# Resident tiles last, bank by bank, and the work on single nodes in groups of four tiles

## The chip, the cores and the metric

The kernel runs on one core of a Trainium2 chip. The metric is the device time of one execution in microseconds (us). Every execution leaves records, so each run also gives its span and the clock that TensorE was granted.

## The reference, cut to what matters

Four graph layers over N = 2708 nodes of 128 features share one dense adjacency matrix A (2708 x 2708, float32). 2708 rows are 21 full tiles of 128 and one of 20.

```python
# layer 0: z from A, the 4 nearest neighbours of z, then A plus those neighbours
z  = leaky_relu(lap_mul(A, x) @ W1 + b1, 0.1)
S  = exp(-sqrt(dist2(z, z)) / 2), kept for the 4 nearest of each row, else 0
x  = layernorm(x + lap_mul(S + A, x) @ W2 + b2)
# layer 1: attention; num = A @ exp(leaky_relu(row + col)); H = A @ (att @ XW)
x  = layernorm(x + H)
# layer 2: normalized A times x, a linear layer
x  = layernorm(x + (d * (A @ (d * x))) @ W.T + b)
# layer 3: A times x beside x itself, a linear layer, relu
x  = layernorm(x + relu(concat(x, A @ x) @ W.T + b))
```

So there are five products with A of 128 columns ("passes": two in layer 0, one each in layers 1, 2 and 3), one more for the attention, a search for neighbours with a gather of their rows, and the attention's own stage ("heads").

## The kernel before

Six of the 22 tiles of A stay in SBUF (`res`), sixteen are streamed in each pass through three buffers. A pass sums into six PSUM banks of 512 columns, `accs`; two spare banks (`mis`) serve all small products. Resident and streamed tiles alternate, and all banks end together:

```python
def adj_times(y, extra=None):
    accs = [acc_tile() for _ in range(C)]
    for n, i in enumerate(order):            # two streamed, one resident, ...
        src = res[:, i, :] if i < RES else load_strip(i)
        for c in range(C):
            nc.tensor.matmul(accs[c][:, : cw[c]], lhsT=y[: pw[i], i, :], rhs=src[...],
                             start=(n == 0), stop=(n == T - 1 and extra is None))
    for c in range(C):
        if extra is not None:
            extra(c, accs[c])
        evacuate(c, hT[...], accs[c][...])   # VectorE and ScalarE in turn
```

The work on single nodes follows for all tiles at once; for the end of layer 0 and the gather before it:

```python
for t in range(T):                 # 22 tiles x 4 neighbours = 88 gathers by GpSimd
    for k in range(TOPK):
        got = knn2.tile([P, D], F32, tag="got", name="got", bufs=16)
        nc.gpsimd.indirect_dma_start(out=got[:p, :], in_=y2_rows[:, :], ...)
        ... near_sum[:, t, :] += sim * got          # VectorE
adj_times(y2, add_near)            # add_near adds near_sum into the banks at the pass's end
add_bias(b2_sb)
for t in range(T):
    ... linear, xs update, stats(t)
normalize()                        # one root for all 22 tiles
... per tile: transpose, products with the attention's weights, column, masks for a ranking
```

In the heads, 22 groups of rows are worked on twice, once for each half of the columns; the result of a half is copied out by VectorE:

```python
for h in range(2):
    hacc = ops.tile([P, 3 * CW], F32, tag="hacc", name="hacc")
    for q in range(NQ):
        ...                        # rows, num, mix: Ln and Exp on ScalarE, three operations on VectorE
    nc.vector.tensor_copy(hT[:, h * HALF : (h + 1) * HALF], hacc[:, :HALF])
```

## Time and profile before

| | us |
|---|---|
| timed runs | 1467.51, 1468.24, 1473.81 |
| the profiled run | 1403.67 (span 1402.0) |
| first pass begins / first search / last search ends | 107.2 / 261.1 / 392.8 |
| first / last gather begins | 407.7 / 521.3 |
| attention product, heads | 612.1 to 745.1, 749.2 to 997.6 |
| passes of layers 1, 2, 3 begin | 1007.0, 1130.4, 1250.7 |

The end of the second pass in the timeline of TensorE shows who sets it (start, duration, engine, line, operation, count, and in brackets the idle time before it with what ended it):

```profile
484.02 18.53 PE L147 MATMUL acc<-strip,y 128*128 128x512 f32 x48
502.48 5.91 PE L340 MATMUL acc<-ident,near_sum 128*128 128x128 f32 x36
...
519.38 0.80 PE L340 MATMUL acc<-ident,near_sum 128*128 128x128 f32 x2 [4.56 <-DVE near_sum L331]
```

The 48 matmuls run without a break up to 502; then TensorE waits for the sums of gathered rows.

### The profile page before, as it was taken

The numbers are of one execution on the slowest core, as the hardware profiler recorded it, in microseconds if no ns is written. First come the engines' busy times: TensorE is split into PE (matmuls) and PEld (weight loads), VectorE is DVE, ScalarE is ACT, GpSimd is POOL, SyncE is SP. The second block draws the span as 40 slices with busy tenths as digits, with TensorE's granted clock in tenths as the row PEclk, the third lists the DMA queues.
The fourth block names the chain that finished last, engine by engine and source line by source line (L and its number), as shares of the span: only waits on it lengthen the run. The fifth ranks groups of instructions, "written<-read, shape, count | busy, mean of one in ns | idle before, by whom it ended". The sixth has DMA issues, their size and how long they took to land.

```text
span 1402.0 us, 10710 instructions
## 1 busy us (share of the span) xinstructions
PE 1160.5 (83%) x3635; PEld 546.2 (39%) x3635; DVE 676.7 (48%) x1261; ACT 264.6 (19%) x519; POOL 230.3 (16%) x232
## 2 busy tenths in 40 slices
PE   0029995999959967668998999999899879989995
PEld 0024443344424435424333333333344434454453
DVE  3860005699942238984004999877500330060025
ACT  0000001455510002301203665444100000000001
POOL 0000000000027770002304564443000000000000
PEclk9999995899989975579899999999799889979975
DMA  8974551000047710233443453343365435535511
GB/s 331 387 300 159 212 193 37 1 0 0 1 136 259 243 43 1 92 148 134 144 165 94 149 171 96 109 133 119 124 232 187 176 123 195 184 138 200 204 40 41
DMA packets 44463, 199.74 MB, mean 142 GB/s; under 512 B 12512, under 2 KB 22114, under 8 KB 30054
## 3 DMA queue, kind: packets, MB, share of 16 engines
q1 hardware_dynamic: 19352, 157.74, 30.7%
q0 software_dynamic: 17280, 36.31, 8.7%
q10 hardware_dynamic: 7770, 4.95, 1.2%
q8 instruction: 30, 0.49, 0.1%
q14 instruction: 31, 0.25, 0.1%
HBM read 223.21 MB, written 4.16 MB: 162 GB/s over the span
## 4 chain that ended last, share of the span: by engine, by line
PE 48%; DVE 20%; issue 12%; DMA 11%; POOL 6%; ACT 1%; POOLq 0%; ACTq 0%; SPq 0%; DVEq 0%
PE acc L147 29%; PE acc L648 7%; DVE where L297 5%; DVE near L296 5%; DMA got<-y_rows,where 4%; POOL rows L703 4%; DMA strip<-in_adjT 3%; PE num L716 3%; PE hacc L640 2%; POOL got L323 1%; DVE colsum L218 1%; PE mis L766 1%; DVE xs L180 1%; PE mis L207 1%; DMA xs<-in_x 1%
## 5 line engine op out<-in xcount | busy, mean ns | idle before, releaser
L147 PE MATMUL acc<-strip,y 128*128 128x512 f32 (+3 forms) x576 | 227.6, 552 | 29.1 <-DVE y L164 14.8
L128 DVE COPY hT<-acc 128x512 f32<-128x512 f32 x15 | 10.2, 688 | 391.5 <-PE acc L147 391.5
L147 PEld LDWEIGHTS acc<-strip,y 128*128 128x128 f32 (+1 forms) x576 | 106.6, 193 | 148.5 <-issue 133.2
L323 POOL DMA_INDIRECT got<-y_rows,where x88 | 88.0, 1000 | 432.7 <-PE acc L147 406.2
L703 POOL DMA_INDIRECT rows<-in_adjT,slot_i x86 | 117.3, 1364 | 174.5 <-PE num L716 104.1
L716 PE MATMUL num<-rows,lw 128*64 128x512 f32 (+2 forms) x516 | 132.7, 558 | 6.3 <-DMA rows<-carry 4.2
L640 PE MATMUL hacc<-err,xws 128*128 128x512 f32 (+3 forms) x264 | 118.5, 573 | 3.3 <-DVE err L635 3.2
L126 ACT COPY hT<-acc 128x512 f32<-128x512 f32 (+1 forms) x15 | 7.3, 485 | 562.6 <-PE acc L147 436.0
L294 PE MATMUL acc<-zT,z 128*128 128x512 f32 (+2 forms) x264 | 106.0, 550 | 0.0
L633 DVE TENSOR_TENSOR err<-inv,num 128x1024 f32<-128x1024 f32 (+1 forms) x88 | 74.3, 854 | 33.5 <-ACT inv L630 32.9
L221 PE MATMUL mis<-ones,colsum 128*128 128x1 f32 (+1 forms) x44 | 9.3, 345 | 93.8 <-DVE colsum L218 93.8
L629 ACT ACTIVATE inv<-num 128x1024 f32<-128x1024 f32 (+2 forms) x88 | 64.3, 735 | 113.5 <-PE num L716 111.5
L147 PE MATMUL acc<-res,y 128*128 128x512 f32 x216 | 84.7, 542 | 0.0
L648 PE MATMUL acc<-strip,lc 128*86 128x512 f32 (+1 forms) x192 | 81.0, 563 | 1.0 <-DVE lc L522 1.0
L295 ACT COPY key<-acc 128x512 f32<-128x512 f32 (+1 forms) x132 | 68.5, 536 | 59.2 <-issue 31.1
L640 PEld LDWEIGHTS hacc<-err,xws 128*128 128x128 f32 (+1 forms) x264 | 45.2, 190 | 87.8 <-issue 48.2
L635 DVE SCALAR_TENSOR_TENSOR err<-gb,g_inv,err 128x1024 f32<-128x1024 f32 (+1 forms) x88 | 78.8, 916 | 0.0
L147 PE MATMUL acc<-strip,mixed 128*128 128x512 f32 (+1 forms) x192 | 76.4, 552 | 0.0
L147 PE MATMUL acc<-strip,xs 128*128 128x512 f32 (+1 forms) x192 | 75.6, 551 | 0.0
L634 DVE SCALAR_TENSOR_TENSOR err<-err,inv 128x1024 f32<-128x1024 f32 (+1 forms) x88 | 73.5, 856 | 0.0
L294 PEld LDWEIGHTS acc<-zT,z 128*128 128x128 f32 (+1 forms) x264 | 47.2, 185 | 59.5 <-issue 59.5
L716 PEld LDWEIGHTS num<-rows,lw 128*64 128x64 f32 (+1 forms) x516 | 39.4, 136 | 79.3 <-issue 60.7
(215 smaller groups left out, 1272.1 us busy)
## 6 DMA issues: line engine op xcount, KB each, us to landing
strip<-in_adjT SPq DMA_DIRECT2D x105, 1354.0 KB
res<-in_adjT SPq DMA_DIRECT2D x6, 1354.0 KB
strip<-in_adjT SPq DMA_DIRECT2D x7, 211.6 KB
got<-y_rows,where POOLq DMA_INDIRECT x88, 3.9
rows<-in_adjT,slot_i POOLq DMA_INDIRECT x86, 6.1
rows<-carry SPq DMA_DIRECT2D x86, 10.6 KB
y_rows<-y ACTq DMA_DIRECT2D x1, 1344.0 KB
xw_rows<-xwe ACTq DMA_DIRECT2D x1, 1344.0 KB
```

Of the source, the lines that this page charges most:

```text
L147: nc.tensor.matmul(accs[c][:, : cw[c]], lhsT=y[: pw[i], i, :], rhs=src[: pw[i], c * CW : c * CW + cw[c]], start=(n == 0), stop=(n == T - 1 ...
L294: nc.tensor.matmul(pks[c][:p, : cw[c]], lhsT=z2[:, :p], rhs=zT[:, cs], start=False, stop=True)
L296: nc.vector.max(near[:p, t, :], key[:p])
L297: nc.vector.max_index(where[:p, t, :], near[:p, t, :], key[:p])
L323: nc.gpsimd.indirect_dma_start(out=got[:p, :], out_offset=None, in_=y2_rows[:, :], in_offset=bass.IndirectOffsetOnAxis(ap=where[:p, t, k : ...
L633: nc.vector.tensor_mul(err[:p], inv[:p], num[:p, :w])
L634: nc.vector.scalar_tensor_tensor(err[:p], err[:p], 2.0, inv[:p], op0=ALU.subtract, op1=ALU.mult)
L635: nc.vector.scalar_tensor_tensor(err[:p], gb[:p, col : col + w], g_inv[:p, q : q + 1], err[:p], op0=ALU.max, op1=ALU.mult)
L640: nc.tensor.matmul(haccs[:, o:e], lhsT=xws[:p, q, :], rhs=err[:p, o:e], start=(q == 0), stop=(q == NQ - 1))
L648: nc.tensor.matmul(accs[c][: 2 * NB, : cw[c]], lhsT=lc[: pw[i], i, :, :].rearrange("p b s -> p (b s)"), rhs=src[: pw[i], c * CW : c * CW + ...
L703: nc.gpsimd.indirect_dma_start(out=rows[:KC, n, :], out_offset=None, in_=adj_half[:, :], in_offset=bass.IndirectOffsetOnAxis(ap=slot_i[h][ ...
L716: nc.tensor.matmul(num[n * BJ : n * BJ + bw[b], o:e], lhsT=lw[:, b, : bw[b]], rhs=rows[:, n, c0 + o : c0 + e], start=True, stop=True,)
```

## The change

The intent: in the end of a pass TensorE works on resident tiles, which need no transfer, one bank after the other. As a bank ends, its four tiles of nodes can be finished on the other engines beside the matmuls of the next bank. The diff, cut to its core:

```diff
-            for c in range(C):   # all banks, tile by tile, to the end
+        for n, i in enumerate(list(lead) + [i for i in range(S) if i not in lead]):
+            src = lead[i] if i in lead else load_strip(i)          # 16 streamed tiles first
+            for c in range(C):
+                add(c, i, src, n == 0, False)
         for c in range(C):
+            for i in range(S, T):                                  # then 6 resident, bank by bank
+                add(c, i, res[:, i - S, :], False, i == T - 1 and extra is None)
             if extra is not None:
                 extra(c, accs[c])
-            evacuate(c, hT[...], accs[c][...])
+            nc.scalar.copy(hT[...], accs[c][...])
+            done(c, chunk_tiles[c])                                # that bank's four tiles
...
-    for t in range(T): linear, xs, stats(t)
-    normalize()
+    def end_layer0(c, ts): linear, xs, normalize(ts), transposes, products, masks
-            pc = acc_tile()
+            pc = mis_tile()
...
+                if t == T - 6:
+                    weigh(range(0, T - 5))     # weights of 17 tiles inside the search
+            weigh(range(T - 5, T))             # the row writes now from SyncE's queue
...
-    gb = wide.tile([P, N], F32, tag="gb", name="gb")
+    gb = hT
-                nc.vector.tensor_copy(hT[:, h * HALF : (h + 1) * HALF], hacc[:, :HALF])
+                nc.scalar.copy(mT[:, h * HALF : (h + 1) * HALF], hacc[:, :HALF])
...
+    for t in range(T): own3 = x @ wx + bias    # layer 3's own part, ahead of its banks' ends
+    def end_layer3(c, ts): linear, relu, normalize(ts, last), store of these tiles
```

The resident tiles are now the last six of the 22, not the first six, so all 16 streamed tiles are full ones. The first pass begins with the three strips that the column sums before it left in the buffers (`lead`), so it fetches 13. The ends of layers 1 and 2 become functions of a group of tiles in the same way, the constants of the ranking are formed early, and the attention product takes its resident tiles last.

## The prediction

> **What bounds the kernel now.** The kernel runs one core, so only a time to beat matters: 1468.24 us median, while the profiled execution spans 1402.0 us. I reason in the profile's time and carry a difference over one to one; the 66 us between the two I take as unchanged, since nothing in the profile explains it.
>
> I read the page's busy shares and its 40 slices first, then cut the span into stages with the view of windows, then read the order of instructions on TensorE, VectorE, ScalarE and GpSimd in the timeline.
>
> ```profile
> PE 1160.5 (83%) x3635; PEld 546.2 (39%) x3635; DVE 676.7 (48%) x1261; ACT 264.6 (19%) x519; POOL 230.3 (16%) x232
> ...
> PEclk9999995899989975579899999999799889979975
> ```
>
> TensorE is busy 83% of the span, but not evenly: the slices where its granted clock is 5 to 7 lie between the dense passes. The windows give those stages exactly. Columns: busy us (and instructions) of PE, weight loads, DVE, ACT, POOL, then granted clock, DMA share, GB/s.
>
> ```profile
> 107.00:209.00 102.00, 101.82 (x264) 48.02 (x264) 1.55 (x4) 1.17 (x2) 0.00 (x0) 1.00 0.54 192
> 209.00:261.00 52.00, 30.91 (x111) 17.73 (x110) 25.17 (x103) 11.70 (x37) 0.00 (x0) 0.57 0.08 28
> 256.00:393.00 137.00, 130.07 (x391) 57.04 (x390) 131.14 (x67) 72.34 (x151) 0.00 (x0) 0.99 0.00 0
> 502.50:523.90 21.40, 7.97 (x43) 7.00 (x42) 5.70 (x18) 1.17 (x2) 15.39 (x17) 0.67 0.15 39
> 523.90:541.00 17.10, 14.08 (x46) 10.41 (x46) 16.70 (x82) 0.51 (x2) 1.85 (x28) 0.50 0.01 1
> 541.00:598.00 57.00, 35.61 (x319) 25.98 (x319) 53.68 (x148) 18.75 (x69) 0.00 (x0) 0.50 0.21 73
> 1110.00:1130.40 20.40, 7.56 (x23) 3.77 (x22) 19.98 (x92) 1.79 (x3) 0.00 (x0) 0.51 0.20 72
> 1232.60:1250.70 18.10, 14.29 (x52) 10.30 (x51) 17.49 (x82) 1.04 (x4) 0.00 (x0) 0.62 0.23 81
> 1352.40:1402.00 49.60, 29.86 (x106) 21.06 (x104) 26.69 (x113) 5.73 (x22) 0.00 (x0) 0.50 0.10 29
> ```
>
> Line 1 is one product with the adjacency: 264 matmul instructions, TensorE full for 102 us at clock 1.00, everything else asleep. Four such passes exist, and each is followed by a tail in which all 22 tiles of nodes are worked on while no adjacency matmul runs: 52 us after the first (to the first key search), 21 + 17 + 57 us after the second, then 20, 18 and 50 us. They sum to 235 us. In these tails VectorE is the full engine (20.0 of 20.4 us in layer 1) or a chain of short handshakes is (the last tail: PE 30, DVE 27 of 50 us). The third line, the neighbour search, is VectorE's (131 of 137 us).
>
> The 21 us before 523.9 are another thing: the pass is over, but its sum waits for the last gathered neighbour rows.
>
> ```profile
> 518.77 0.96 POOL L323 DMA_INDIRECT got<-y_rows,where  x1 [0.30 <-issue]
> 520.04 0.94 POOL L323 DMA_INDIRECT got<-y_rows,where  x1 [0.30 <-DMA got<-y_rows,where]
> 521.28 0.96 POOL L323 DMA_INDIRECT got<-y_rows,where  x1 [0.30 <-DMA got<-y_rows,where]
> ```
>
> 88 gathers start 1.30 us apart from 407.69 to 521.28: GpSimd sets the pace, and the gather outlasts the pass by 21 us.
>
> [...] 0.50 in the tails, 1.00 in the passes; and a pass after a tail pays for the release (its first 19 instructions took 9.76 us from 1130.42, where dense ones take 0.379 us each, 7.2 us). [...] in the attention product of the kernel before (624 to 655 us) placing matmuls and product matmuls do alternate without idle time, so the scheduler does this. [...] strips, row writes and gathers in the second pass; the trace shows 225 GB/s at a share of 0.66 there.
>
> **The change part by part.** A pass now takes 16 streamed strips first, then for each of 6 banks its 6 resident tiles, then that bank's copy and its four tiles' end work. Matmul count does not change, nor do weight loads (the row of busy shares has as many loads as matmuls, 3635 each), so no cost there. A pass stays 264 x 0.379 = 100 us: 73 us of strips, then 27 us of resident matmuls, 4.55 us per full bank, beside which end work can run.
>
> 1. First tail (52 us). TensorE's own part, 30.9 us at clock 0.57, becomes some 12 us of warm time for the linear products and transposes (the part of it that belongs to the search is not counted), inserted into the 27 us. VectorE needs about 1.04 us per tile plus some ten tiny operations per bank, 5.7 us, against about 6.7 us of TensorE per bank: it keeps up. What stays after the last bank is the chain of two tiles: copy 0.28, linear 0.3, z operations 1.0, transpose and copy 0.5, splitting of the norms 2.2, transpose and copy 0.5, last search matmuls and copy 1.2, with handshakes about 7 us. Plus 3 us for places where the static order guesses wrong: 22 us stay. Saved 30.
> 2. The search: weights for 17 tiles are now formed inside it. On VectorE that is five operations of 0.2 to 0.3 us and a row scaling of 17/22 x 3.09 = 2.4 us: cost 3.4 us, as VectorE sets the pace there.
> 3. From the last search to the first gather: now 392.8 to 407.7, 14.9 us, with a scaling of 3.09 and a write of 1344 KB that took 5.97. Only 5 tiles remain: scaling 0.7, the write an estimated 3 plus up to 1 behind a strip on the same queue. Saved 4. The second pass itself can start some 12 us earlier, for its first 16 tiles are ready, but that does not set the end: the gather does, 114 us plus landing, unchanged.
> 4. Layer 0's end, 523.9 to 597 us, 73 us with VectorE busy 70. The intent is that banks 0 to 4 do theirs while the gather runs. VectorE's part per bank is about 9 us rising to 18 (masks of 0.34 to 2.99 us). But it also sums the gathered rows, in a fixed order. In the kernel before, all copies of the bank ends stand behind the last gathered row on VectorE, and ScalarE's scaling of the later gather is ordered as if a gather took about half its real time. So I expect the compiled order to put most of layer 0's end behind the gather. Central: an overlap of 8 us, given back by bubbles at six group ends. Saved 0.
> 5. Setup constants move to idle time, the ranking after 598 keeps its operations, the heads are untouched: 0. The attention product keeps its length.
> 6. Layer 1: 20.4 us becomes 22 warm transposes of 0.2 us and 2 us of stalls. The next pass begins with tiles 0 to 15, long ready. Saved 14.
> 7. Layer 2: 18.1 us against 22 linear products of 0.29 us. Saved 11. Passes 3 and 4 also start warm: 2.4 + 2.0 us, saved 4.
> 8. Layer 3: 49.6 us becomes 15 us of warm TensorE (half of 30) and a last chain of 11: copy and product 1, backlog of bank 4 on VectorE 3, two tiles and their root 3.3, store 3.7 as at the end now. Saved 23.6.
>
> Sum: 30 - 3.4 + 4 + 0 + 14 + 11 + 4 + 23.6 = 83. I take off 5 us for strips that come late: while streaming, a strip of 1354 KB is eaten in 4.55 us, which is 305 GB/s, where a pass of the kernel before drew 192. The first 94 us of the trace sustain 357 GB/s, so it should nearly fit. Net 78: 1468 - 78 = 1390 us, a profiled span near 1324.
>
> **Rivals.**
> A: the strips become the bound. In the second pass gather (about 50 GB/s in small pieces) and row writes come on top of 305 GB/s, near 357. For it: three buffers only. Against it: each has 9.1 us to be refilled, and in the second pass the gather ends later anyway. If 3 passes lost 8 us each: 1410.
> B: layer 0's end really overlaps the gather. VectorE is 76% free during it and banks 0 to 4 need some 65 us; banks reach their end about 45 us before the gather does. That would save 25 to 30 more: 1362.
> C: the fixed order hurts. TensorE stalls on bank c's linear product (two spare banks only) with bank c+1 queued behind, and the clock falls to half in the resident phase. 10 us lost per pass in four passes: 1430. Against it: the tight interleaving cited above[...].
>
> **Range and chances.** Items 1, 6, 7, 8 are the firm part, 83 us with the warm starts; their errors are some 5 us each. Item 4 is open by -12 to +28, A and C pull up. I put 1390, with 1360 to 1420 for 8 in 10. 2% is 29 us, reached by layers 1 to 3 alone: faster 0.95, same 0.04, slower 0.01.
>
> **What would show it.** Right: the clock stays near 1.00 from the start of layer 1's pass to the end of layer 3's; layer 2's pass starts within 1 to 3 us of the last matmul of layer 1's; a last tail near 11 us; first search about 122 us after the first pass began (now 154); gathers still 1.30 us apart and starting about 10 us after the last search; VectorE full for about 70 us after the last gathered row. Wrong: idle TensorE before strip matmuls, put down to the strip's DMA (A); VectorE doing masks before the gather's end (B); matmuls of 128x512 at twice 0.379 us in the resident phases (C).

## More of the kernel before

Several chips served the runs, and what they had in common and what not is a part of the story.

## The result, and the profile after

The kernel after takes 1340.11 us (median of four runs, 1338.74 to 1345.34) where the kernel before took 1471.03 (1467.51 to 1474.62) beside it. The ratio is 0.9116, with a 95% interval of 0.9079 to 0.9154. It is 131 us faster, 53 us more than predicted, and below the range.

The profiled run is one of the timed ones (1338.74 us). From its page, the lines that answer to those of before:

```profile
PE 1110.0 (83%) x3635; PEld 511.7 (38%) x3635; DVE 675.9 (51%) x1349; ACT 293.5 (22%) x586; POOL 244.4 (18%) x254
...
PEclk9999998999998777856979899999989999999999
```

The same matmuls take 50 us less of busy time, for fewer of them run at half clock (the mean granted clock is 0.932, 0.896 before): in the last third, where before has three slices at 7 and one at 5, all but one stand at 9 now, and that one at 8. Its windows by stage (the columns are those of the prediction's windows):

```profile
107.00:230.00 123.00, 119.10 (x352) 55.05 (x352) 27.32 (x129) 11.41 (x31) 0.00 (x0) 0.98 0.49 181
230.00:240.00 10.00, 9.98 (x23) 3.64 (x24) 2.72 (x18) 4.55 (x14) 0.00 (x0) 0.69 0.00 1
388.00:511.00 123.00, 67.15 (x148) 29.94 (x146) 29.07 (x88) 0.00 (x0) 87.92 (x88) 0.77 0.47 161
511.00:606.00 95.00, 70.03 (x452) 43.29 (x453) 69.67 (x210) 22.17 (x79) 0.00 (x0) 0.72 0.13 45
1106.30:1213.60 107.30, 107.30 (x309) 51.43 (x308) 22.10 (x105) 6.42 (x18) 2.68 (x6) 1.00 0.57 207
1213.60:1329.30 115.70, 115.66 (x375) 58.63 (x374) 29.71 (x143) 10.22 (x35) 0.00 (x0) 1.00 0.45 165
1329.30:1337.00 7.70, 0.81 (x4) 0.41 (x4) 4.58 (x26) 0.69 (x3) 0.00 (x0) 0.67 0.15 44
```

The last three lines are layer 2, layer 3 and the tail: TensorE full at clock 1.00 from pass to pass, then 7.7 us where 49.6 stood. The third and fourth line are the surprise: TensorE is busy 67 of 123 us while the gather runs, and layer 0's end behind it takes 95 us, not 73.

But the two profiles differ by 65 us and the timed runs by 131. So the first thing to find was what the timed runs of the kernel before do that its profile does not show.

### The profile page after: what moved, and what is told of

It reads as the page before. It is cut to its first block, busy times and chain, and to the rows that moved or that the text cites. A ratio compares the mean times of both kernels' runs of the same rounds, so it can differ in the third digit from the quotient of the medians.

```text
span 1337.0 us, 10860 instructions
## 1 busy us (share of the span) xinstructions
PE 1110.0 (83%) x3635; PEld 511.7 (38%) x3635; DVE 675.9 (51%) x1349; ACT 293.5 (22%) x586; POOL 244.4 (18%) x254
## 4 chain that ended last, share of the span: by engine, by line
PE 69%; DVE 10%; issue 6%; DMA 6%; POOL 5%; POOLq 2%; ACT 1%; another core or an unknown queue 0%; ACTq 0%; DVEq 0%; SPq 0%
PE acc L139 32%; PE num L741 7%; PE acc L667 7%; PE hacc L659 7%; PE acc L387 7%; POOL got L407 4%; DVE mask L474 2%; DMA strip<-in_adjT 2%; DVE colsum L219 2%; PE acc L384 2%; POOLq L407 2%; PE mis L205 1%; DMA xs<-in_x 1%; DVE where L390 1%; DMA res<-in_adjT 1%
## 5 line engine op out<-in xcount | busy, mean ns | idle before, releaser
L139 PE MATMUL acc<-strip,y 128*128 128x512 f32 (+1 forms) x576 | 229.9, 560 | 53.9 <-DMA strip<-in_adjT 29.6
L139 PEld LDWEIGHTS acc<-strip,y 128*128 128x128 f32 x576 | 107.1, 197 | 175.0 <-issue 138.5
L139 PE MATMUL acc<-res,y 128*128 128x512 f32 (+1 forms) x216 | 98.2, 562 | 2.1 <-issue 1.9
L667 PE MATMUL acc<-strip,lc 128*86 128x512 f32 x192 | 84.3, 578 | 0.9 <-DVE lc L546 0.9
L648 ACT ACTIVATE inv<-num 128x1024 f32<-128x1024 f32 (+1 forms) x88 | 64.4, 736 | 83.7 <-PE num L741 80.2
L139 PE MATMUL acc<-strip,xs 128*128 128x512 f32 x192 | 77.2, 544 | 0.0
L654 DVE SCALAR_TENSOR_TENSOR err<-hT,g_inv,err 128x1024 f32<-128x1024 f32 (+1 forms) x88 | 77.0, 916 | 0.0
L139 PE MATMUL acc<-strip,mixed 128*128 128x512 f32 x192 | 75.5, 554 | 0.0
L387 PEld LDWEIGHTS acc<-zT,z 128*128 128x128 f32 (+1 forms) x264 | 47.7, 188 | 59.0 <-issue 58.4
L389 DVE MAX8 near<-key 128x8 f32<-128x2708 f32 (+1 forms) x22 | 65.5, 2979 | 6.1 <-ACT key L388 6.1
L649 ACT ACTIVATE inv<-inv 128x1024 f32<-128x1024 f32 (+1 forms) x88 | 67.2, 768 | 2.6
```

Source lines behind the costliest of these rows:

```text
L387: nc.tensor.matmul(pks[c][:p, : cw[c]], lhsT=z2[:, :p], rhs=zT[:, cs], start=False, stop=True)
L649: nc.scalar.activation(inv[:p], inv[:p], AF.Exp, scale=-1.0)
L654: nc.vector.scalar_tensor_tensor(err[:p], gb[:p, col : col + w], g_inv[:p, q : q + 1], err[:p], op0=ALU.max, op1=ALU.mult)
L667: nc.tensor.matmul(accs[c][: 2 * NB, : cw[c]], lhsT=lc[: pw[i], i, :, :].rearrange("p b s -> p (b s)"), rhs=src[: pw[i], c * CW : c * CW + ...
```

## The experiments

### What are the 66 us between profile and timed runs?

**Run 1**, the kernel before once more, unchanged but for a comment.

> The kernel before, unchanged: what are the 66 us by which its timed runs (1467 to 1474 us) exceed its profiled one (span 1402)? Theory H (the heads have two paces): in the profile each step of the head stage took 4.90 us up to about 870 us and 6.08 us from there on; if the timed runs hold the slow pace, all 44 steps, from about 760, cost some 26 us more than the profile shows (22 steps x 1.18 us). Then a profile of a 1470 us execution shows head steps of 6 us or more throughout, and the stage takes 275 us or more (249 in the first profile, 227 in the kernel after). Theory P (the profile itself is faster or the gap is spread): a profiled execution again spans about 1402 while the timed ones span 1467 to 1474, or all stages are longer by the same 4.7%. Then the heads alone do not carry it.

Measured: 1468.49 us (1456.28 to 1474.6), ratio 1.0035 (0.996 to 1.011), and now the profile is of such an execution, with a span of 1467.2 us. The heads take 250 us in it, as in the first profile (248): the theory of the heads falls as an explanation of the gap, though a slow half is there in both. The place is the second pass. TensorE's timeline:

```profile
445.29 1.71 PE L147 MATMUL acc<-res,y 128*128 128x512 f32 x3
449.20 0.85 PE L147 MATMUL acc<-res,y 128*128 128x512 f32 x1 [2.20 <-issue]
452.01 1.01 PE L147 MATMUL acc<-res,y 128*128 128x512 f32 x1 [1.96 <-issue]
454.81 1.01 PE L147 MATMUL acc<-res,y 128*128 128x512 f32 x1 [1.78 <-issue]
...
561.67 19.48 PE L147 MATMUL acc<-strip,y 128*128 128x512 f32 x48
```

From 446 us TensorE often takes only one matmul each 2.80 us (seven in a row from 449 to 466), where dense ones come 0.379 us apart, and it waits for nothing that the profile shows ("issue"). These are operands long resident. In the records of GpSimd's queue (the views don't list them), small register and semaphore instructions that last 17 or 29 ns during the gather of the first profile last 685 to 712 ns in 48 places of the same stretch. I call this the crawl. It begins after 26 of 88 gathers and ends with the last of them; the pass ends at 581 instead of 503. The first profile shows not one such instruction. Something else goes with it: of 5,611 records of landed transfers in the first profile this one holds 3,994. They go missing before the crawl begins: up to the first gather both profiles hold 876, from there to the 25th gather 384 and 86.

Of the 65 us between the two spans, 55 lie from the first gather to the attention product, and 6 from the first pass to the first search. The 6 are not the crawl: run 5 below has none and takes 158.9 us there, run 1 159.9, and the first profile 153.9.

How much of the pass was done explains the cost. Adjacency matmuls of the second pass (of 264) started before the 25th gather, and before the last gathered rows had landed (2.5 us after the last gather began):

| | before the 25th gather | before the last rows landed | pass begins ahead of the first gather |
|---|---|---|---|
| before, first profile (no crawl) | 98 | 264 | 7.3 us |
| before, run 1 (crawl) | 94 | 157 | 7.3 us |
| after (crawl) | 140 | 204 | 22.8 us |
| after, run 9 below (no crawl) | 140 | 208 | 22.5 us |

The kernel before in the crawl has 107 matmuls left when the gather ends. The kernel after crawls too, and there it shows as strips that come late:

```profile
440.92 6.52 PE L139 MATMUL acc<-strip,y 128*128 128x512 f32 x12 [20.10 <-DMA strip<-in_adjT]
454.73 6.44 PE L139 MATMUL acc<-strip,y 128*128 128x512 f32 x12 [7.29 <-issue]
470.46 7.11 PE L139 MATMUL acc<-strip,y 128*128 128x512 f32 x12 [9.29 <-DMA strip<-in_adjT]
488.19 6.78 PE L139 MATMUL acc<-strip,y 128*128 128x512 f32 x12 [10.62 <-issue]
```

Yet it has as many matmuls done at the gather's end as the same kernel without the crawl (204 and 208). So the crawl costs it little there. SyncE issued these strips at 434, 449, 464 and 482 us, with the DMA engines used to 33 to 43% over these stretches of 15 to 20 us, and to 15% from 421 us until the first of them: it is the issue that is late, not the transfer; what holds SyncE I could not settle.

**Runs 2 and 3** asked whether the attention product's order sets the pace of the heads (the kernel before with the new order, the kernel after with the old one).

```diff
 # run 2, in the kernel before (run 3: the reverse, in the kernel after)
-    for n, i in enumerate(order):
+    for n, i in enumerate([*range(RES, T), *range(RES)]):
```

> The kernel before, with one thing of the change: the attention product takes its 16 streamed tiles first and the 6 resident ones last, so that all three stream buffers are free some 25 us before that product ends and the first rows of the heads come early. Theory H2 (the heads fall into the slow pace because their rows start late): the heads run at 4.9 us a step throughout, and the time falls to about 1400 us or below (1468 minus 66). Rival (placement of buffers or the copy of the heads' result sets the pace): the time stays at 1462 to 1474, within 8 us of the kernel before.

> The kernel after, with the attention product's old order (two streamed, one resident, alternating). Theory H2: the heads fall into the slow pace, in some executions or in all; time 1340 becomes 1360 to 1405. Rival: stays at 1335 to 1347, and the heads' pace is owed to something else in the change.

Measured: run 2 took 1461.98 us (ratio 0.9995, 0.9943 to 1.0046), run 3 1347.21 (0.9225, 0.9179 to 0.927). The heads stay at 247.5 and 228.9 us. The order of that product is not it.

**Run 4**, a rival for the late strips: the row writes that share SyncE's queue with them.

```diff
-            nc.sync.dma_start(y2_rows[...], y2[...])
+            nc.scalar.dma_start(y2_rows[...], y2[...])
```

> The kernel after, with the writes of the scaled rows issued by ScalarE as before, not by SyncE. In the second pass of the kernel after, SyncE issued the strips late: TensorE waited 20, 7, 9 and 11 us for single strips while the DMA engines were used to 14 to 20%. Theory Q (the row writes on SyncE's queue hold the strips back): TensorE's waits for strips in the second pass vanish, the first bank ends near 470 instead of 503 us, and some of layer 0's end moves into the gather: 1340 becomes 1320 to 1330. Rival (SyncE waits for something else, or the gather sets the end anyway): the waits stay, time 1337 to 1347.

Measured: 1343.05 us (0.9191, 0.9146 to 0.9237). The four strips are issued about as late as before (at 427, 443, 463 and 478 us), and TensorE waits 43 us for them, where it waited 47. Theory Q falls. (The 14 to 20% of the expectation are shares of the DMA engines before a strip's issue alone.)

### The heads

**Runs 5 and 6** exchange one line: who copies a half's result.

```diff
 # run 5, in the kernel before (run 6: the reverse, in the kernel after)
-                nc.vector.tensor_copy(hT[:, h * HALF : (h + 1) * HALF], hacc[:, :HALF])
+                nc.scalar.copy(hT[:, h * HALF : (h + 1) * HALF], hacc[:, :HALF])
```

> The kernel before, with one line of the change: the copy of a half's result of the heads is made by ScalarE, not VectorE. In three profiles of the kernel before, every step of the heads' second half took 6.09 us where those of the first took 4.76 to 4.90; in the kernel after (and two variants of it) both halves ran at 4.90. Theory S (the copy's engine at the half's end changes the order in which the second half's instructions stand on the engines, and so its pace): second half at about 4.90 us a step, time 1463 minus 20 x 1.19 = 24 us, so 1435 to 1445. Rival (the places of the buffers, which the change moved too, set the pace): second half stays at 6.09 us, time 1455 to 1474.

> The kernel after with that one line turned back: VectorE copies a half's result. Theory S: second half at about 6.09 us a step, 1340 becomes 1358 to 1368. Rival (buffers): both halves stay at 4.90, time 1335 to 1347.

Measured: run 5 took 1387.9 us where the kernel before took 1412.53 on that chip (0.9831, 0.9784 to 0.9877), 24.6 less; its heads' second half runs at 4.90 us a step. (The interval is clear of 1 but reaches across 2%; the expected 1435 to 1445 was meant for a chip with the crawl, and the difference is the 24 us named.) The heads themselves take 230.0 us, and 247.5 to 250.4 in the four profiles of the kernel before, or a variant of it, with the old line, so they hold 18 to 20 of the 24.6 us. Run 6 took 1345.57, with steps of 6.09 us in the second half and heads of 248.8 us; without the turned line 1322 was measured (run 9, another chip without the crawl). Theory S holds from both sides. Windows of 90 us in the second half; first run 1 (the old line, VectorE copies), then run 5 (the new one), with the columns as above:

```profile
960.00:1050.00 90.00, 89.90 (x268) 28.28 (x266) 71.64 (x90) 41.59 (x60) 34.20 (x25) 1.00 0.39 119
```

```profile
890.00:980.00 90.00, 88.33 (x314) 33.06 (x312) 88.36 (x110) 52.93 (x71) 43.30 (x30) 1.00 0.47 150
```

In 90 us VectorE does 90 operations with the old line and 110 with the new one. In the old it is busy 80% and waits for ScalarE once a step (18.4 us in 15 waits in that window; 0.8 us in 2 with the new line): the compiled order of the second half is another one, and makes a chain through both engines. The first profile shows both orders; first a step of its first half, then one of its second half, where ScalarE does the two logarithms (L629) before the two exponentials (L630) and VectorE waits for the last:

```profile
825.24 1.02 ACT L629 ACTIVATE inv<-num 128x1024 f32<-128x1024 f32 x1 [0.79 <-PE num L716]
826.29 1.06 ACT L630 ACTIVATE inv<-inv 128x1024 f32<-128x1024 f32 x1
828.39 0.45 ACT L629 ACTIVATE inv<-num 128x330 f32<-128x330 f32 x1 [1.04 <-PE num L716]
828.87 0.48 ACT L630 ACTIVATE inv<-inv 128x330 f32<-128x330 f32 x1
```

```profile
942.46 0.45 ACT L629 ACTIVATE inv<-num 128x330 f32<-128x330 f32 x1 [2.92 <-PE num L716]
943.29 1.02 ACT L629 ACTIVATE inv<-num 128x1024 f32<-128x1024 f32 x1 [0.39 <-PE num L716]
944.21 1.41 ACT L630 ACTIVATE inv<-inv 128x330 f32<-128x330 f32 x2
944.71 0.50 DVE L633 TENSOR_TENSOR err<-inv,num 128x330 f32<-128x330 f32 x1 [1.24 <-ACT inv L630]
```

Why the compiler orders it so after this copy, I have not looked into.

These were also the first runs with a kernel before of 1412.53 us (1405.7 to 1418.07), and no profile of this call has a crawl or lacks records (5,593 to 5,609 of landed transfers). In all, two chips ran without the crawl (kernel before 1412.5 and 1414.6 us) and three with it (1463.2, 1470.5, 1462.7), each in all its runs. The runs of the first result had it too, by the profile of the kernel after and by the times of the kernel before; on which chip the first profile was taken I do not know. Of the 18 profiles ten have the crawl, with 3,751 to 4,046 records of landed transfers, and eight neither it nor a gap (5,593 to 5,611). No run here is without records, so whether the missing ones have to do with its cause is open, as is why a chip has it or not.

### What the change is worth in either kind

**Run 7** takes the early start of the second pass away. It was run twice, the second time (run 13) on a chip with the crawl.

```diff
-                if t == T - 6:
-                    weigh(range(0, T - 5))
-            weigh(range(T - 5, T))
+            weigh(range(T))
```

> The kernel after, but the weights are formed once, after the whole search, so that the second pass cannot start before the search is over (it started 24 us earlier, at 365 us, than the first gather). In ordinary executions TensorE and GpSimd crawl from about the 25th gather to the last one, so what the pass has done by then counts. Theory E (the early start of the second pass is worth its full length, for in ordinary executions that pass and not the gather sets the end): the pass starts some 25 us or more later, some 6 fewer strips are done when the crawl begins, and time rises by 20 to 45 us, to 1360 to 1385. Rival (the gather sets the end, as the prediction had it): only the longer gap before the gathers shows, plus the 3.4 us of weights that leave the search: 1337 to 1346.

> The kernel after with the weights formed once, after the search. Without the crawl it took 1322.6, as the kernel after does. With the crawl (before at about 1465): theory E: some 40 matmuls fewer are done before the 25th gather, and 1340 becomes 1352 to 1375. Rival (slack enough even so): 1335 to 1347.

**Run 9** is the kernel after, unchanged.

> The kernel after, unchanged, once more. So far two kinds of executions were seen, and each chip showed only one: with a crawl (TensorE and GpSimd take an instruction every 0.7 or 1.4 us from about the 25th gather to the last; some 1,600 of 5,600 records of landed transfers are missing; kernel before 1463 to 1471, kernel after 1340), and without (kernel before 1412 timed, 1402 in the first profile; variants of the kernel after 1322 to 1346). Theory K (the prediction read a profile without the crawl, the timed runs had it; without it the change is worth nearly what was predicted, 78 us): where before takes about 1410, after takes 1318 to 1335, a difference of 78 to 95; where before takes about 1465, after takes 1335 to 1347. Rival (the change is worth some 130 us on any chip): after is 1275 to 1290 where before is 1410.

Measured: run 9 takes 1322.05 us where before takes 1414.61: 92.6 us, ratio 0.9341 (0.9305 to 0.9377). Theory K holds, its rival falls. Run 7 without the crawl takes 1322.64 (0.9378 against its own kernel before): the early start is worth nothing there, as the prediction had it, since the gather ends later anyway. Run 13 with the crawl takes 1363.08 (0.9269, 0.9244 to 0.9294), about 23 us more than the 1340.11 of the kernel after on another such chip; only 96 matmuls were done at its 25th gather and 148 at the last landing. Theory E holds with the crawl, its rival without.

**Run 12** is the kernel before with 40 gathers. Its output is wrong, which doesn't matter for the time.

```diff
+                if t < 10:
                     ... gather into a new got, kept[k] = got
+                got = kept[k]
```

> The kernel before with 40 gathers instead of 88 (wrong result on purpose: the later tiles sum the rows of tile 9 again). Without the crawl: the gather ends some 62 us earlier, before the pass does, so the 21 us in which the pass's sum waited for the last rows go: 1412 becomes 1388 to 1396. With the crawl, theory G (the crawl belongs to the gathers: on from about the 25th, off with the last): it lasts 20 us instead of 90, and 1465 becomes 1395 to 1420. Rival (the crawl, once on, lasts as long as the pass): 1445 to 1465.

Measured: 1422.07 us, before 1470.47 (0.9677, 0.9655 to 0.97), on a chip with the crawl. Small instructions of GpSimd are slow from the 25th gather to the last at 469 us, and TensorE then does the 155 matmuls left after 471.5 in the 60.9 us up to 532.4, 0.39 us each. The crawl belongs to the gathers. (The time is 2 us above theory G's range.)

### Layer 0's end and the tails

**Run 8** puts the ends of layers 1 to 3 behind all six banks, **run 10** that of layer 0 (run 17 is run 10 again).

```diff
             nc.scalar.copy(hT[...], accs[c][...])
-            done(c, chunk_tiles[c])
+            if not whole:
+                done(c, chunk_tiles[c])
+        if whole:
+            for c in range(C):
+                done(c, chunk_tiles[c])
```

> The kernel after with the ends of the passes of layers 1 to 3 taken whole: residents still last, bank by bank, but the work on single nodes stands behind all six banks. The prediction's steps 6, 7 and 8 with the warm starts make 52.6 us. If they hold and come from the work lying beside the banks: 1340 becomes 1385 to 1400, with tails near 20, 18 and 50 us again. Rival (part of the gain comes from bank-wise order alone, for example since only the last tiles wait for their bank, and the scheduler lays work beside banks anyway): 1345 to 1370.

> The kernel after with layer 0's end behind all six banks (residents still bank by bank). Prediction's step 4 put the grouping of layer 0's end at 0. In the profiles without the crawl it costs: TensorE stood 39 us before bank 0's linear products until VectorE had summed the last gathered row, with the residents of banks 1 to 5 queued behind. Theory W (the groups cost more than they hide): without them the residents are done while the gather runs, and 12 to 20 us are saved. Rival: same within 6 us, or slower by up to 15 where the crawl is on, since fewer instructions are left behind it.

> The base for the run before: layer 0's end whole, again. Without the crawl 1318 to 1325. With the crawl not measured yet; an estimate is 1325 to 1345, as the residents are then not held up behind layer 0's end.

Run 8: 1344.16 us (0.9522, 0.9477 to 0.9567), so 22 us more than the kernel after without the crawl (run 9, on another chip; run 7, on this one, took 1322.64), not 52: the rival holds. The profile shows why: the passes of layers 2 and 3 begin 5.7 and 4.9 us after the last matmul of the pass before them, with the first groups of four normalized, and the other groups' transposes stand among the next pass's strips. Only the last tail, 25.6 us instead of 7.7, has no next pass to hide beside. So what run 8 keeps (groups of four, residents last, the bank copies by ScalarE, layer 3's own part taken out of the tail; these were not tested one by one) makes 34.7 of the 58.4 us that layers 1 to 3 gained between the first profile and run 9 (from the start of layer 1's pass to the end: 395.0, 360.3 in run 8, 336.6), and the work beside the banks the other 23.7, of which 15.4 are layer 3's.

Run 10: 1322.06 us without the crawl (0.9338), the same as the kernel after; theory W falls. Run 17 with the crawl: 1371.16 us (0.9371, 0.9324 to 0.9418), some 31 us more than the 1340.11 of the kernel after (another chip with the crawl), and above the 1325 to 1345 that its expectation estimated. Its trace shows why: as the last rows land, 60 adjacency matmuls are left (204 of 264 are done), and VectorE stands still until they are through and the first linear product comes (waited for, total us, times, longest):

```profile
DVE xs L455 <- PE mis L209: 32.4, 5, 31.0
```

The kernel after has as many left, but with its groups bank 0's end lies beside them. So the groups of layer 0 cost nothing without the crawl and save with it. Run 9's timeline shows what they wait for, as the prediction's step 4 said:

```profile
506.11 1.22 PE L205 MATMUL mis<-w,hT 128*128 128x128 f32 x4 [56.77 <-DVE xs L451]
507.12 4.83 PE L139 MATMUL acc<-res,y 128*128 128x512 f32 x6
```

TensorE stands 56.8 us at the third of bank 0's linear products (the first two fill the two spare banks), with the residents of later banks behind them, until VectorE has summed the last gathered row.

In run 10 all residents are done during the gather, and still the attention product begins 107 us after the last sum, where 88 passed in the kernel before. VectorE is busy for the same time in both, 84.4 of 107.1 us and 84.2 of 88.1, so the loss is waiting. The waits of VectorE in layer 0's end (waited for, total us, times, longest): first the kernel before, then run 10.

```profile
DVE mask L462 <- ACT xwe L453: 0.6, 2, 0.3
```

```profile
DVE mask L478 <- ACT xwe L469: 13.1, 16, 1.8
```

**Run 16** is run 17 with the transposed column of a tile given an accumulator bank again, as before the change.

```diff
-            pc = mis_tile()
+            pc = acc_tile()
```

> Layer 0's end taken whole, and the transposed column of each tile again in one of the six accumulator banks. In the profile with the whole end VectorE waited 0.3 to 0.7 us in most tiles for ScalarE's copy of the tile's products (13.1 us in 16 waits; 0.6 us in the kernel before). Theory M (two spare banks for three products of a tile make a chain of handshakes): those waits vanish and 10 to 20 us are saved against the whole end without this: 1322 becomes 1302 to 1312 on a chip without the crawl. Rival (normalizing by groups of four costs it): within 5 us of the whole end.

Measured on the chip of run 17, with the crawl: 1362.41 us against 1371.16, so 8.8 us less, and the waits of VectorE for those copies fall from 8.9 us in 13 to 4.7 in 6. The two spare banks for three products are a part of it: 8.8 of the 20 us that layer 0's end lost, if the size carries over from a chip with the crawl; theory M had it at 10 to 20. The rest is open.

### A version that beats both

**Run 11** makes VectorE's fixed order take bank 0's end earlier: the sums of the gathered rows live in two tiles of one bank each, so the third bank's sums must wait until the first bank's are used.

```diff
-    near_sum = sum_pool.tile([P, T, D], F32, tag="near_sum", name="near_sum")
-    for t in range(T): gathers and sums
+    def gather(c):
+        sums[c] = sum_pool.tile([P, 4, D], F32, tag="near_sum", name="near_sum", bufs=2)
+        for t in chunk_tiles[c]: gathers and sums
+    for c in range(2):
+        gather(c)
     def add_near(c, acc):
         ... lhsT=sums[c][:p, t - ts[0], :]
+        if c + 2 < C:
+            gather(c + 2)
```

> The kernel after, with the sums of the gathered rows kept in two small tiles of one bank each instead of one tile of 22, so that VectorE's fixed order must put bank 0's end before the sums of the later banks. In the compiled order bank 0's end now stands after the sums of 12 tiles (48 of 88 gathers) and bank 1's among those of the rest. Theory V (VectorE's fixed order alone kept layer 0's end out of the gather): 20 to 40 us saved, 1290 to 1302 where the kernel after takes 1322. Rival (gathers now wait for free sums, and end later by as much as is won): within 8 us of the kernel after.

> The kernel after with the sums of the gathered rows by bank, again. Without the crawl 1299 again, against 1410 to 1415 of the kernel before. With the crawl: the work moved into the gather crawls too, so less or nothing is won: 1318 to 1345 where the kernel after takes 1340.

Measured without the crawl: 1299.19 us (0.9191, 0.9157 to 0.9225), 23 less than the kernel after on the same chip (1322.05). The gathers end no later (last one at 503.3, 502.7 in run 9), and layer 0's last mask ends at 574 instead of 598. Theory V holds. With the crawl (run 15): 1344.97 us (0.9164, 0.9131 to 0.9197), nothing won over the 1340 of the kernel after: the 49th gather waits 27.3 us, until TensorE has used bank 0's sums at 481 us, and the last one begins at 541. GpSimd's slow instructions end at 450 us in this run, before that pause, and do not come back: "to the last gather" does not hold here.

## Why the prediction was wrong

The stages, in us saved, worked out from starts of one stage to the next in two pairs of profiles: first profile of before (1402.0) against run 9 (1320.0), without the crawl; run 1 (1467.2) against the first profile of after (1337.0), with it.

| step of the prediction | predicted | without crawl | with crawl |
|---|---|---|---|
| 1 first tail (first pass to first search) | 30 | 19.9 | 26.9 |
| 2 weights in the search | -3.4 | -3.4 | -3.4 |
| 3 last search to first gather | 4 | 2.5 | 2.3 |
| 4 first gather to attention product | 0 | -20.1 | 25.9 |
| 5 attention product and heads | 0 | 25.2 | 18.1 |
| 6 and 7 layers 1 and 2, warm starts | 29 | 30.5 | 32.3 |
| 8 layer 3 to the end | 23.6 | 27.9 | 28.4 |
| late strips | -5 | 0 | in step 4 |
| start of the first pass | 0 | -0.5 | -0.3 |
| sum | 78 | 82.0 | 130.2 |

Two rows differ between the kinds for other reasons than the second pass. In row 1 it is the first profile, shorter there by 5 us than run 5, which has no crawl either. In row 5 it is the attention product of the kernel after: it takes 141.2 us with the crawl (140.7 to 142.8 in seven profiles of it and its variants) and 132.1 without (132.1 to 132.5 in six), which was not looked into.

**The step that failed** stands in the first paragraph: "I reason in the profile's time and carry a difference over one to one; the 66 us between the two I take as unchanged". The profile was of an execution without the crawl, the timed runs had it. With the crawl the wait that ends last in the second pass is another: item 3 says of the pass that it "does not set the end: the gather does", but in run 1 the pass ends at 581, 46 us after the last gather began. The crawl lengthened the stretch from the first gather to the attention product from 204.4 to 259.8 us in the kernel before, and from 224.5 to 234.0 in the kernel after. The change hides most of it: the second pass starts 15 us earlier against the gathers (22.5 us ahead of the first one, not 7.3; run 13 lost 23 us without that), and layer 0's end is grouped (run 17 lost 31 us without that; both were on other chips with the crawl, and no run takes both away). Had the kinds been the same, the change in the profile would have been right to 4 us (82 against 78), but by luck in part: errors of 10 to 25 us in items 1, 4 and 5 cancel. And the first profile is short even for its kind: its 1403.67 us lie below all 14 timed runs without the crawl (1405.7 to 1418.39). By the medians the change is worth 92.6 us without the crawl (run 9), which is 15 more than predicted and inside the range.

**Step 1** had the mechanism right and a size wrong. The resident phase is as tight as said: TensorE ends the pass 115 us after its start, against 112 expected. But the rest is 19 us, not 10: the last bank holds 148 columns and its residents take 2 us, so the end of bank 4's four tiles had nothing left to lie beside. I had counted such a backlog in step 8 and forgot it here.

**Step 2** is exact (131.7 to 135.1 us). **Step 3** saved less, since the gap is 12.4 us and not 11; its second half, that the early start "does not set the end: the gather does", is right without the crawl and wrong with it.

**Step 4** named the mechanism, VectorE's copies and sums in a fixed order behind the last gathered row, and the trace shows it. Its size was wrong without the crawl: "overlap of 8 us, given back by bubbles" is a loss of 20. VectorE's work was read rightly, about 70 us (69.1 busy in run 9), but it takes 92 us, since VectorE waits between. It is not the grouping (run 10) but the end itself, 8.8 us of it from the third small product on two spare banks (run 16), the rest open. Rival B was open in the hardware and closed by the order: run 11 gets 23 us of it.

**Step 5**, "the heads are untouched: 0", is wrong. One line in them was in the diff, and it is worth 24.6 us in time (run 5), 18 to 20 of them seen in the heads' own stage. I read it as a copy that moves to an idle engine, of no consequence, and had seen the slow second half of the profile without asking what set it.

**Steps 6 to 8** came within 2 and 5 us without the crawl, but not for the reason given alone: run 8, with the work on nodes behind all six banks, still has 34.7 of their 58.4 us. The clock is 0.98 to 1.00 over layers 1 to 3, layer 2's pass begins with the last matmul of layer 1's (not 1 to 3 us later), and the last tail is 7.7 us, not 11. In the first profile layer 2's pass ran at clock 0.50 for its first 4.0 us and layer 3's for its first 3.1, and both at 1.00 from there: that is the loss behind the warm starts (9.76 us for 19 matmuls in layer 2, not 7.2). (The text counts four passes; its own list of tails has the five that there are, and no number hangs on the word. It gives the clock in the tails as 0.50; its own windows show 0.50 to 0.67.) The **late strips** cost nothing without the crawl: the first pass of run 9 takes its 192 streamed matmuls without one wait, at 271 GB/s, with three of the 16 strips in the buffers beforehand; in the passes of layers 1 and 2, which fetch all 16, TensorE is busy throughout (105.9 of 105.9 and 107.4 of 107.4 us).

Of the rivals, A (strips as the bound) shows in the second pass with the crawl alone, but is caused by late issues, not by the transfers. C came in layer 0's second pass alone: TensorE stands 56.8 us with the spare banks full, and the first six matmuls behind take 4.83 us, over twice 0.379 each; run 10 takes that stall away and gains nothing without the crawl. In the other passes it did not come.

## What to carry to other kernels

When the profiled run is shorter than all timed runs, find out first what it lacks, before any difference is carried from one to the other: an overlap that looks worthless in the one may be the largest gain in the other. The signs here were records missing from the first gather on, and, from about the 25th of 88 gathers to the last (in run 15 only to the 43rd), small instructions of 0.7 or 1.4 us on GpSimd and in run 1 a matmul each 2.80 us on TensorE. Give each operation of a diff the question which engine's order it changes, even a copy at the end of a loop; and look at the pace of a loop by its halves, for a mean hides that one of them runs at 6.09 and the other at 4.90. An end need not lie beside its own pass: with groups of four the next pass can start with the first group, and run 8, built so, kept over half of the gain of layers 1 to 3. Putting the end beside its own pass's matmuls paid most where no next pass follows (15.4 of 23.7 us), and nothing where an engine's fixed order held it back (run 10, without the crawl).
